# Two attention layers with MLPs on one core: the division by the softmax totals is moved from VectorE to ScalarE and GpSimd

## The chip, the cores and the metric

The kernel runs on one core of a Trainium2 chip. The time is the device time in microseconds (us) of one execution; several executions are timed and the median is given. A profile is one execution recorded by the hardware profiler, whose span runs from its first to its last instruction. The engines are named as in the profile: PE is TensorE (matmuls; PEld is its weight loads), DVE is VectorE, ACT is ScalarE, POOL is GpSimd, SP is SyncE, which here only issues transfers. [...]

## The reference

The input x has 4 sequences of 1024 rows of 256 numbers, all float32. Four blocks follow each other, each added to x after a layernorm.

```
x = x + attn_a(layernorm(x))   # 16 heads of 64, scale 1/(64*64*16), output weights WO
x = x + ffn(layernorm(x))      # 256 -> 1024, gelu, 1024 -> 256, with biases
x = x + attn_b(layernorm(x))   # own layernorm, low-rank q and k/v, rotary q and k, residual inside
x = x + ffn(layernorm(x))

# in both attention layers, for each sequence and head
scores = q @ k.T * scale
attn   = softmax(scores, axis=-1)
out    = attn @ v
```

The softmax is computed as exp(score - row maximum), and the division by the row's total is put off until after the product with v: out = (exp @ v) / total.

## The kernel before, in words

Each attention layer is cut into 32 pairs of heads (4 sequences, 8 pairs each) and each pair into 8 steps of 128 query rows, so there are 256 steps in a layer. The order on every engine is written out by hand in `steps_with` (L324): the loop over steps calls the stages of different steps in a fixed order, and each engine runs its instructions in the order in which they were issued.

A step s has these stages. `scores` (L229) makes the two heads' 128x1024 scores on TensorE, into one of three double banks. `exponentials` (L244) takes the row maximum on VectorE (L249) and the exponential on ScalarE (L251), with the row total as a by-product. `invert` (L257) takes the reciprocal of the totals on VectorE (L259), and ScalarE spreads it into a seventeenth column block of the probabilities (L260). `turn` (L265) transposes the probabilities in squares of 32x32 on VectorE (L271), the inverse totals along with them, into a buffer T.

Two steps make a half-pair h, called a round here (HB = 2). `send` (L282) moves T to a buffer pT in sixteen transfers that exchange the squares between partitions: eleven are issued by SyncE in the odd step, after the transpose, and five by GpSimd in the following even step. T and pT have two buffers each. Five steps after its first step (LAG = 5), `weigh` (L290) multiplies the exponentials in pT with v on TensorE (L297), into two banks of PSUM, one for each step of the round. Then `divide` (L303) multiplies each bank by the inverse totals, which are found in pT beside the exponentials (`pT[h][:, :, :, NK2, :]`), and writes oT (L307). When pT has been read there its buffer is free for the sends of the round two later. In the next, even step `project` (L312) multiplies oT with the output weights on TensorE (L167), ScalarE copies the result (`got`, L320), and GpSimd adds it to x (L322).

In an odd step TensorE runs the scores of the next step, then weigh; in the even step that follows it runs the scores of one more step and then project, with no other work between weigh and project than these scores. VectorE runs two maxima, the transpose, and in an odd step the division, before the next reciprocal.

Work for later pairs is spread as "pieces" over the steps: q, k and v of the next pair (copies of their banks on ScalarE, L535, L537, L548 in layer A, L640, L661 in B), and the layernorm and transposes of the next sequence (L147, L153, L156). In layer B the rotary embedding is such a piece: GpSimd issues two transfers that swap neighbouring rows of q or k (`change`, L645), in an odd step, and in the next even step it does three element-wise operations on 128x512 (`rotate`, L650 to L652). One such set falls into each round. GpSimd also adds the layernorm's result to x for the next sequence (L596), and b2 to x in the MLP (L388, 128x256).

In the names of the profile, `sc` is the scores, `p` the probabilities, `mm` a bank of PSUM for matmul results, and `nmax` the negated row maximum.

Of the kernel before, what the change touches and what calls it, by code (L numbers as in the profile page):

```python
# [11 lines left out]
ALU = mybir.AluOpType  # L12
# [13 lines left out]
SQ = 32  # L26
NG = P // SQ
HB = 2
# [5 lines left out]
NK2 = S // DH  # L34
# [5 lines left out]
def hybrid_block_kernel(  # L40
# [5 lines left out]
    nc = tc.nc  # L46
# [134 lines left out]
    def attention(prep_batch, prep_pair, wo, loader, lead):  # L181
# [22 lines left out]
        n = len(steps)  # L204
# [22 lines left out]
        sc, probs, total, T, pT, av, oT = {}, {}, {}, {}, {}, {}, {}  # L227

        def scores(s):  # L229
            g, qs = steps[s]  # L230
            qT, kT = tiles[g]["qT"], tiles[g]["kT"]
            for j in range(2):
                sc[s, j] = ps_sc.tile([P, S], F32, tag="sc", name="sc")
            for m in range(S // 512):
                for half in range(2):
                    for j in range(2):
                        rows = slice(j * DH, (j + 1) * DH)
                        nc.tensor.matmul(  # L238
                            sc[s, j][ts(half, DH), ts(m, 512)],
                            qT()[rows, ts(2 * qs + half, DH)], kT()[rows, ts(m, 512)],  # L240
                            start=True, stop=True,
                        )

        def exponentials(s, j):  # L244
            if j == 0:
                probs[s] = pp.tile([P, NK, NG, SQ], F32, tag="p", name="p")
                total[s] = small.tile([P, 2], F32, tag="total", name="total")
            nmax = small.tile([P, 1], F32, tag="nmax", name="nmax")
            nc.vector.tensor_reduce(nmax, sc[s, j], AX.X, ALU.max, negate=True)  # L249
            place = j ^ (s % HB)  # L250
            nc.scalar.activation(  # L251
                probs[s][:, :NK2, ts(j, 2), :],
                sc.pop((s, j)).rearrange("p (k c i) -> p k c i", c=2, i=SQ), AF.Exp,
                bias=nmax, accum_out=total[s][:, place : place + 1],
            )

        def invert(s):  # L257
            t = total.pop(s)
            nc.vector.reciprocal(t, t)  # L259
            nc.scalar.copy(  # L260
                probs[s][:, NK2].rearrange("p (j c) i -> p j (c i)", j=2),
                t.unsqueeze(2).to_broadcast([P, 2, DH]),
            )

        def turn(s):  # L265
            h, q = divmod(s, HB)
            if q == 0:
                T[h] = tp.tile([P, SENT], F32, tag="T", name="T").rearrange(
                    "p (c q k i) -> p c q k i", c=NG, q=HB, k=NK
                )  # L270
            nc.vector.transpose(  # L271
                T[h][:, :, q, :, :].rearrange("p c k i -> p k c i"), probs.pop(s)
            )
# [8 lines left out]
        def send(h, engine, which):  # L282
            if h not in pT:
                pT[h] = ptp.tile([P, SENT], F32, tag="pT", name="pT").rearrange(
                    "p (a q k i) -> p a q k i", a=NG, q=HB, k=NK
                )
            for a, c in which:
                engine.dma_start(pT[h][ts(c, SQ), a], T[h][ts(a, SQ), c])  # L288

        def weigh(h):  # L290

            v = tiles[HB * h // NT]["v"]()
            av[h] = [group(P) for q in range(HB)]
            for k in range(NK2):
                for q in range(HB):
                    for j in range(2):
                        nc.tensor.matmul(  # L297
                            av[h][q][ts(j ^ q, DH)], v[ts(j, DH), k, :],
                            pT[h][ts(j, DH), :, q, k, :],
                            start=(k == 0), stop=(k == NK2 - 1),  # L300
                        )

        def divide(h):  # L303
            oT[h] = otp.tile([P, HB, P], F32, tag="oT", name="oT")
            R = pT.pop(h)[:, :, :, NK2, :]
            for q, sums in enumerate(av.pop(h)):
                nc.vector.tensor_tensor(  # L307
                    oT[h][:, q].rearrange("p (a i) -> p a i", i=SQ),
                    sums.rearrange("p (a i) -> p a i", i=SQ), R[:, :, q], op=ALU.mult,
                )  # L310

        def project(h):  # L312
            g, t0 = divmod(HB * h, NT)
            b, pr = pairs[g]
            po = group(HB, D)
            for t in range(HB):
                paired(po[:, t, :], [(oT[h][:, t], [wos[g][:, t]] * 2)])
            oT.pop(h)
            got = tmp.tile([P, HB, D], F32, tag="tmp", name="got")
            nc.scalar.copy(got, po)  # L320
            xd = xs[b][:, t0 : t0 + HB, :]
            nc.gpsimd.tensor_add(xd, xd, got)  # L322

        def steps_with(others):  # L324
            for k, f in others:
                pieces.setdefault(k, []).append(f)
            for s in range(-1, n + LAG + 1):
                h, part = divmod(s - LAG, HB)
                ahead = 0 <= s + 1 < n
                if 0 <= s < n:  # L330
                    invert(s)
                if ahead:
                    scores(s + 1)
                if part == 1 and 0 <= s // HB - 1 < n // HB:
                    send(s // HB - 1, nc.gpsimd, squares[len(squares) - POOL_DMA :])
                    T.pop(s // HB - 1)
                if part == 1 and 0 <= h < n // HB:
                    project(h)
                if ahead:
                    exponentials(s + 1, 0)  # L340
                for f in pieces.get(s - EARLY, ()):
                    f()
                if part == 0 and 0 <= h < n // HB:
                    weigh(h)
                if ahead:
                    exponentials(s + 1, 1)
                if 0 <= s < n:
                    turn(s)
                if part == 0 and 0 <= h < n // HB:
                    divide(h)  # L350
                if part == 0 and 0 <= s < n:
                    send(s // HB, nc.sync, squares[: len(squares) - POOL_DMA])
                for f in pieces.get(s, ()):
                    f()
# [394 lines left out]
```

## Time and profile before

| | us |
|---|---|
| median of three runs | 3321.29 (3320.86 to 3324.8) |
| the profiled execution's own time | 3321.26 |
| its span | 3319.5 |
| VectorE busy | 2626.0 (79%) |
| ScalarE busy | 1892.7 (57%) |
| GpSimd busy | 1774.2 (53%) |
| the division, L307, 512 instructions | median 0.270 each |

The span has four parts: attention A up to about 1420 us, an MLP, attention B from about 1650 to 3090 us, and the last MLP. Busy shares are means over all four, so a stage is read from its own stretch. An instruction's row in a group gives its line, engine, operation, operands, shape and count, then busy time and mean duration, then the idle time of its engine ahead of it and what ended most of that idle time. A row of the timeline gives the start, the duration, the engine, the line and the operands, and in brackets how long the engine had been idle and what released it. The ends of matmuls are modelled by the profiler. TensorE can have matmuls in the records whose intervals overlap.

### The profile page before, as it was taken

Reading aid. Unit: us, or ns where it says so; the run is one execution under the profiler, and the core shown is the slowest. Engines: PE = TensorE matmul, PEld = TensorE weight load, DVE = VectorE, ACT = ScalarE, POOL = GpSimd, SP = SyncE. Lnnn points to the kernel's source line nnn. Section 1 sums busy time; section 2 is a strip of 40 time slices with the busy share of each in tenths; the row PEclk is TensorE's granted clock in tenths of the full one; section 3 lists DMA queues with packets and bytes.
Section 4 is the critical chain, followed back from the end, with each engine's and each line's share of the span. In section 5 each row is a group of like instructions: output and inputs, shape, how many; then the busy total and the mean of one; then the engine's idle time right before and its main releaser. Section 6 shows DMA issues by size and latency. Waiting matters only on the chain.

```text
span 3319.5 us, 124467 instructions
## 1 busy us (share of the span) xinstructions
PE 3241.7 (98%) x52608; PEld 2028.1 (61%) x52608; DVE 2626.0 (79%) x2898; ACT 1892.7 (57%) x3664; POOL 1774.2 (53%) x2482
## 2 busy tenths in 40 slices
PE   8999999999999999999999999999999999998999
PEld 4666666666666666666655655656556656665666
DVE  7998998899988999931069988999899989999100
ACT  5666666665666666643356665666566666665332
POOL 3444444344444444321257887888778878886100
PEclk9999999999999999999999999999999999999999
DMA  8888888888888888830049888998899889998100
GB/s 225 224 218 218 223 224 219 219 220 222 228 212 221 220 225 222 221 82 0 7 126 243 240 241 242 250 248 242 232 247 251 241 235 251 251 254 228 41 20 19
DMA packets 250825, 659.82 MB, mean 199 GB/s; under 512 B 76352, under 2 KB 105024, under 8 KB 250272
## 3 DMA queue, kind: packets, MB, share of 16 engines
q1 hardware_dynamic: 167248, 415.43, 48.0%
q0 software_dynamic: 83024, 236.44, 25.2%
q8 instruction: 418, 6.85, 0.9%
q14 instruction: 135, 1.11, 0.1%
HBM read 43.39 MB, written 4.19 MB: 14 GB/s over the span
## 4 chain that ended last, share of the span: by engine, by line
PE 70%; DVE 9%; SPq 7%; DMA 6%; issue 3%; ACT 3%; POOL 1%; DVEq 0%; ACTq 0%; POOLq 0%
PE sc L238 20%; PE mm L297 18%; PE mm L167 14%; PE mm L413 7%; SPq L288 7%; PE ph L402 6%; DVE T L271 5%; DMA pT<-T 5%; PE mm L176 4%; DVE nmax L249 3%; ACT p L251 1%; PE mm L153 1%; POOL pT L288 1%; DVE oT L307 0%; ACT gT L406 0%
## 5 line engine op out<-in xcount | busy, mean ns | idle before, releaser
L249 DVE TENSOR_REDUCE nmax<-sc 128x1 f32<-128x1024 f32 x1024 | 1202.8, 1216 | 171.1 <-PE sc L238 161.1
L251 ACT ACTIVATE p<-sc,nmax 128x1024 f32<-128x1024 f32 x1024 | 1144.0, 1117 | 329.1 <-DVE nmax L249 328.2
L271 DVE STREAM_TRANSPOSE T<-p 128x2176 f32<-128x2176 f32 x512 | 1246.7, 2435 | 62.2 <-DMA pT<-T 46.8
L288 POOL DMA_DIRECT2D pT<-T x1280 | 625.3, 496 | 1016.8 <-DVE total L259 775.9
L238 PE MATMUL sc<-kT,qT 64*64 64x512 f32 x8192 | 1109.9, 599 | 18.1 <-ACT p L251 15.3
L297 PEld LDWEIGHTS mm<-pT,v 64*64 64x64 f32 x32768 | 960.1, 133 | 159.2 <-issue 105.1
L297 PE MATMUL mm<-pT,v 64*64 64x128 f32 x32768 | 1009.4, 270 | 12.8 <-issue 11.2
L238 PEld LDWEIGHTS sc<-kT,qT 64*64 64x64 f32 x8192 | 347.4, 133 | 408.6 <-issue 276.5
L260 ACT COPY p<-total 128x128 f32<-128x128 f32 x512 | 152.8, 298 | 509.5 <-DVE total L259 503.1
L322 POOL TENSOR_TENSOR x<-x,got 128x512 f32<-128x512 f32 x256 | 330.5, 1291 | 49.4 <-ACT got L320 45.4
L420 DVE TENSOR_TENSOR x<-x,mm 128x512 f32<-128x512 f32 x32 | 21.9, 686 | 364.7 <-PE mm L413 364.7
L167 PE MATMUL mm<-wo,oT 128*64 128x256 f32 x2048 | 277.8, 392 | 13.4 <-DVE oT L307 12.3
L167 PEld LDWEIGHTS mm<-wo,oT 128*64 128x64 f32 x2048 | 124.3, 136 | 260.4 <-DVE oT L307 151.1
L320 ACT COPY got<-mm 128x512 f32<-128x512 f32 x256 | 150.0, 586 | 226.4 <-PE mm L167 225.5
L406 ACT ACTIVATE gT<-ph,b_sb 128x512 f32<-128x512 f32 x128 | 87.5, 686 | 304.3 <-PE ph L402 304.3
L167 PE MATMUL mm<-hT,w 128*64 128x512 f32 x1024 | 243.7, 597 | 1.0 <-ACT hT L156 1.0
L413 PE MATMUL mm<-w_sb,gT 128*128 128x256 f32 x1024 | 226.0, 381 | 6.6 <-ACT hT L156 6.6
L402 PE MATMUL ph<-hT,w_sb 128*128 128x512 f32 x512 | 229.2, 600 | 0.0
L413 PEld LDWEIGHTS mm<-w_sb,gT 128*128 128x128 f32 x1024 | 193.1, 190 | 39.4 <-ACT hT L156 9.4
L251 ACT ACTIVATION_READ_ACCUMULATOR p<-sc,nmax 128x1 f32 x1024 | 204.4, 200 | 0.0
L388 POOL TENSOR_TENSOR x<-x,b_sb 128x256 f32<-128x256 f32 x64 | 44.5, 726 | 275.2 <-ACT xn L147 275.2
L176 PEld LDWEIGHTS mm<-w,hT 128*64 128x64 f32 x4096 | 140.9, 138 | 71.3 <-issue 69.7
(88 smaller groups left out, 2187.5 us busy)
## 6 DMA issues: line engine op xcount, KB each, us to landing
pT<-T SPq DMA_DIRECT2D x2816, 136.0 KB, 4.7
pT<-T POOLq DMA_DIRECT2D x1280, 136.0 KB, 4.6
turned<-kT POOLq DMA_DIRECT2D x128, 128.0 KB, 3.8
turned<-qT POOLq DMA_DIRECT2D x128, 128.0 KB, 3.9
w<-in_wqkv_a POOLq DMA_DIRECT2D x96, 128.0 KB, 6.1
wo<-in_wo_a POOLq DMA_DIRECT2D x32, 128.0 KB, 5.2
wo<-in_wo_a POOLq DMA_DIRECT2D x64, 64.0 KB, 5.6
wo<-in_wo_b SPq DMA_DIRECT2D x32, 128.0 KB, 4.5
```

What stands on the lines that cost most here:

```text
L167: nc.tensor.matmul(out[ts(j, DH)], lhsT[:, ts(j, DH)], rhs[j], start=(first and i == 0), stop=(last and i == len(parts) - 1),)
L176: nc.tensor.matmul(out[ts(j, DH)], lhsT, rhs[:, ts(j, DH)], start=(i == 0), stop=(i == len(parts) - 1),)
L238: nc.tensor.matmul(sc[s, j][ts(half, DH), ts(m, 512)], qT()[rows, ts(2 * qs + half, DH)], kT()[rows, ts(m, 512)], start=True, stop=True,)
L249: nc.vector.tensor_reduce(nmax, sc[s, j], AX.X, ALU.max, negate=True)
L251: nc.scalar.activation(probs[s][:, :NK2, ts(j, 2), :], sc.pop((s, j)).rearrange("p (k c i) -> p k c i", c=2, i=SQ), AF.Exp, bias=nmax, acc ...
L260: nc.scalar.copy(probs[s][:, NK2].rearrange("p (j c) i -> p j (c i)", j=2), t.unsqueeze(2).to_broadcast([P, 2, DH]),)
L271: nc.vector.transpose(T[h][:, :, q, :, :].rearrange("p c k i -> p k c i"), probs.pop(s))
L288: engine.dma_start(pT[h][ts(c, SQ), a], T[h][ts(a, SQ), c])
L297: nc.tensor.matmul(av[h][q][ts(j ^ q, DH)], v[ts(j, DH), k, :], pT[h][ts(j, DH), :, q, k, :], start=(k == 0), stop=(k == NK2 - 1),)
L322: nc.gpsimd.tensor_add(xd, xd, got)
L402: nc.tensor.matmul(ph, w1_sb[:, c, ts(f, P)], hT[n][:, c, :], start=(c == 0), stop=(c == NC - 1),)
L413: nc.tensor.matmul(po[n][:, t % 2, :], gT[n][:, f, ts(t, P)], w2_sb[:, f, :], start=(f == 0), stop=(f == NF - 1),)
```

## The change

`divide` becomes `take`. ScalarE copies the two banks to oT as they are, and one multiply on GpSimd, over both halves and in place, brings in the inverse totals. The buffer pT is then freed by GpSimd. In the order of the step, `take` is called ahead of `turn` instead of behind it; since `turn` issues on VectorE only, this decides nothing between the two. On ScalarE the two copies stand behind the step's second exponential and ahead of the integer-numbered pieces of the step; on GpSimd the multiply stands ahead of those pieces, the swap transfers L645 among them. Below line 310 the line numbers of the kernel after are lower by one.

```diff
-        def divide(h):
+        def take(h):
+
             oT[h] = otp.tile([P, HB, P], F32, tag="oT", name="oT")
-            R = pT.pop(h)[:, :, :, NK2, :]
             for q, sums in enumerate(av.pop(h)):
-                nc.vector.tensor_tensor(
-                    oT[h][:, q].rearrange("p (a i) -> p a i", i=SQ),
-                    sums.rearrange("p (a i) -> p a i", i=SQ), R[:, :, q], op=ALU.mult,
-                )
+                nc.scalar.copy(oT[h][:, q], sums)
+            parts = oT[h].rearrange("p q (a i) -> p a q i", i=SQ)
+            nc.gpsimd.tensor_mul(parts, parts, pT.pop(h)[:, :, :, NK2, :])
...
                 if ahead:
                     exponentials(s + 1, 1)
+                if part == 0 and 0 <= h < n // HB:
+                    take(h)
                 if 0 <= s < n:
                     turn(s)
-                if part == 0 and 0 <= h < n // HB:
-                    divide(h)
                 if part == 0 and 0 <= s < n:
                     send(s // HB, nc.sync, squares[: len(squares) - POOL_DMA])
```

## The prediction

> **What bounds the kernel now.** I read the page's first part, the windows by stage, the waits of TensorE in each attention layer, the timeline of single rounds, and the groups. A round is two steps: two transposes (L271), one weigh (L297), one division (L307), one projection (L167 from oT). Layer A runs from 60 to 1420 us, layer B from 1690 to 3060 us.
>
> The page, then two stretches of the windows, one in each layer (columns: PE, PEld, DVE, ACT, POOL busy us with instruction counts, clock, DMA share, GB/s):
>
> ```profile
> PE 3241.7 (98%) x52608; PEld 2028.1 (61%) x52608; DVE 2626.0 (79%) x2898; ACT 1892.7 (57%) x3664; POOL 1774.2 (53%) x2482
> ...
> 460.00:860.00 400.00, 399.12 (x7648) 252.83 (x7644) 362.24 (x365) 243.45 (x485) 168.96 (x271) 1.00 0.84 221
> 2080.00:2480.00 400.00, 390.83 (x7007) 240.97 (x7003) 364.84 (x370) 248.74 (x485) 325.75 (x418) 1.00 0.90 243
> ```
>
> In layer A TensorE leaves 0.9 us of 400 idle: VectorE, at 91%, is not what ends a round. In layer B TensorE leaves 9.2 us, VectorE is as full, DMA is at 0.90 and GpSimd at 81%, DMA issues included. The waits of TensorE, layer A first, then B (us, times, longest):
>
> ```profile
> PE mm L297 <- issue: 5.5, 10, 1.2
> PE sc L238 <- ACT p L251: 0.3, 1, 0.3
> PE mm L167 <- DVE oT L307: 0.2, 1, 0.2
> ...
> PE sc L238 <- ACT p L251: 13.0, 13, 2.9
> PE mm L167 <- DVE oT L307: 11.6, 27, 0.5
> ```
>
> The wait that the change bears on, a projection for oT, costs 0.2 us in layer A and 11.6 us in B. So a gain is small; the question is whether the new chain makes this wait large. One round of layer A, from the timeline:
>
> ```profile
> 801.01 3.67 PE L297 MATMUL mm<-pT,v 64*64 64x128 f32 x128
> 803.63 1.12 ACT L251 ACTIVATE p<-sc,nmax 128x1024 f32<-128x1024 f32 x1
> 804.50 1.90 PE L238 MATMUL sc<-kT,qT 64*64 64x512 f32 x16
> 804.64 0.19 ACT L251 ACTIVATION_READ_ACCUMULATOR p<-sc,nmax 128x1 f32 x1
> 805.87 0.45 DVE L307 TENSOR_TENSOR oT<-mm,pT 128x128 f32<-128x128 f32 x2
> 806.33 1.08 PE L167 MATMUL mm<-wo,oT 128*64 128x256 f32 x8
> 806.61 2.46 POOL L288 DMA_DIRECT2D pT<-T  x5 [4.79 <-DVE total L259]
> ```
>
> Let W be the end of a weigh (804.68). TensorE then has only sixteen score matmuls before the projection, which starts at W+1.65. Division starts at W+1.19, after the transpose, and ends at W+1.64. Over the 123 rounds of layer A the medians are the same: first projection load W+1.64, division end W+1.64. The first projection needs only the first half, done 0.18 us earlier. So oT may come 0.2 us later than now before TensorE stalls, and not more. ScalarE is free at W+0.15, GpSimd long before W (median W-4.4).
>
> **The change part by part.** *Removed from VectorE:* 512 multiplies, 0.45 us a pair, 256 pairs: 115 us of its 2626. In A TensorE covers it, worth nothing. The reciprocal (L259) moves up 0.45 us, but the next maximum (L249) waits for scores that end at W+1.72.
>
> *Added to ScalarE:* two 128x128 copies out of PSUM per round. Rows, none with 128 columns from PSUM:
>
> ```profile
> L320 ACT COPY got<-mm 128x512 f32<-128x512 f32 x256 | 150.0, 586 | 226.4 <-PE mm L167 225.5
> L548 ACT COPY v<-mm 128x256 f32<-128x256 f32 x128 | 47.5, 373 | 0.0
> L260 ACT COPY p<-total 128x128 f32<-128x128 f32 x512 | 152.8, 298 | 509.5 <-DVE total L259 503.1
> L388 POOL TENSOR_TENSOR x<-x,b_sb 128x256 f32<-128x256 f32 x64 | 44.5, 726 | 275.2 <-ACT xn L147 275.2
> ```
>
> The first two fall by 213 ns per 256 columns, so 128 columns come to 0.27 us (L260: 0.30). ScalarE's neighbours overlap by 0.10 us, so the pair takes 0.44. Got (L320) starts 0.10 us after its matmul; the exponentials free ScalarE at W+0.15. Copies: W+0.13 to W+0.57. Behind them in ScalarE's queue stand the copy of the inverse (L260), which waits for VectorE until W+1.35 anyway, and, in a few odd steps, a standardisation (L147, 0.6 us) that used to run first. The banks come free earlier than under the division.
>
> *Added to GpSimd:* one 128x256 multiply, in place. The nearest row is L388, 726 ns; 128x512 adds (L322) and multiplies (L650) are within 20 ns of each other, so the operation does not matter. The pattern in runs of 32 elements is not in the trace: I bound it by 0.69 us (L388's start-to-start spacing) and the 128x512 row, 1.29, and take 0.73. Start 0.08 us after ScalarE (the shortest gap from L320 to L322).
>
> *The signal from GpSimd to TensorE* is in no row. Bounds: 0.03 us (VectorE's division to the load) and 0.29 us (from L652 to the transfer L645 that waits for it); from L651 to L652, which also waits, it is 0.08 us. I take 0.1. The Trainium skill, Perfetto Trace Analysis, section GPSIMD Engine Instruction, has GpSimd's reported end at the acknowledged write, with the semaphore visible only after that, and calls such a span unreliable. By the rows oT comes at W+0.57+0.08+0.73+0.10 = W+1.48, in time; with the page's caution read as the 0.29 us row, at W+1.67, which costs 0.02 us a round.
>
> *Shared port.* The same skill, SBUF — State Buffer, section Who interferes with whom, says that GpSimd blocks fully against a VectorE instruction in a two-port mode. VectorE's transpose runs until W+1.2 here. If it held the port, oT would come near W+2.1, at +0.4 us a round, some 100 us in all. The rows speak against it: L650 to L652 take 1.255 to 1.295 us each with transposes beside them. I count nothing.
>
> *Moved on GpSimd's queue.* The multiply waits for W, and everything behind waits with it. Layer A has room (idle 4.8 us before the sends). Layer B, one round with W = 2008.42:
>
> ```profile
> 2005.85 1.27 POOL L652 TENSOR_TENSOR kT<-kT,turned 128x512 f32<-128x512 f32 x1
> 2007.41 1.13 POOL L645 DMA_DIRECT2D turned<-kT  x2 [0.29 <-POOL kT L652]
> 2010.35 2.43 POOL L288 DMA_DIRECT2D pT<-T  x5 [1.81 <-DVE total L259]
> 2012.80 1.29 POOL L322 TENSOR_TENSOR x<-x,got 128x512 f32<-128x512 f32 x1
> 2014.05 1.27 POOL L650 TENSOR_TENSOR kT<-kT,cos_sb 128x512 f32<-128x512 f32 x1
> ```
>
> The swap transfers (L645) go from W-1.0 to W+1.4, the five sends from W+1.9 to about W+2.6, the add to W+5.0, the rotation to W+6.4 and its end to W+10.2. The next multiply can run at W+10.65 at the earliest, in a light round of 10.0 us (projection to projection, 1953.10 to 1963.12). So it fits, with 0.4 us to spare. The swap lands 3.8 us (median; 5.9 at most) after issue, the rotation needs it 4 us after: just covered. SyncE's eleven sends per round wait for the slot of pT and start where they do now, or 0.2 us earlier.
>
> *Layer B.* Gain: the 11.6 us of waits for oT, where VectorE was late, go; of the 13.0 us for exponentials I give 5, since VectorE catches up sooner. Loss: in ten rounds L652 ends later than W+0.5 already, at W+0.5 to W+2.1; adding the multiply and signal to each end and taking what exceeds W+1.65 gives 11 us.
>
> **Sum**: A 0, B -12 -5 +11 = -6 us on the profiled execution's 3321.26 us (span 3319.5 and 1.8 around it), the same as the median of 3321.29: 3315 us.
>
> **The rivals.** *In time, little moves* (0.45): as summed, 3305 to 3322; half of it beyond 0.2% (6.6 us, about what a measurement can tell from no change).
>
> *VectorE relieved in layer B* (0.12): in 37 of 125 rounds VectorE waits under 0.15 us for anything. Shedding 0.45 us there is 17 us, with the 25 us of both waits 40: 3282 to 3305. Against it: 48 us of VectorE's idle time in B lies before the transpose, most of it for transfers of pT (38.7 us), at a DMA share of 0.90, and a light round has a loop without VectorE (scores, projection, got, exponential, scores, weigh) that already takes 10.0.
>
> *oT late in every round* (0.31), the case on the other side: the multiply in pieces, or GpSimd's signal, takes more than assumed. It decides at W+1.65. At W+1.84 (multiply 1.1 us) the excess over all rounds is 26 us in A and 28 more than now in B: 3370 or so with B's relief; at W+1.67 it is about 10 us, 3330. The upper bounds together (1.29 and 0.29, W+2.22) give 141 us; I weigh the lower part most.
>
> *GpSimd's queue binds in B* (0.12): twelve rounds carry two adds L596 (0.73 us each), 10.9 us of work against 10.0 to 10.4; or the rotation waits for its swap. With 0.1 to 0.3 us in each of 125 rounds, 12 to 38 us: 3327 to 3353.
>
> **How the numbers follow.** Faster: 0.12 + half of 0.45 = 0.35. Same: 0.22. Slower: the last two, 0.43. The range cuts the far ends of the second and third case: 3294 to 3358. The likeliest case alone: 3305 to 3322.
>
> **What would show it.** Right: the multiply near 0.73 us, ending near W+1.4; the wait of L167 for GpSimd under 5 us in A; A's rounds still 10.75 us. Wrong: a multiply above 0.9 us, or projections starting after W+1.7 in every round of A; L645 or L650 idle for long in B. VectorE falls by 115 us in any case.

## The result and the profile after

The kernel after takes 3333.6 us (median of 19 runs, 3327.99 to 3341.47), the one before 3324.8 on the same chip (19 runs, 3318.61 to 3329.5). The ratio is 1.0028, 95% interval 1.002 to 1.0035: 9 us slower, where 3315 and a gain were forecast. The time lies inside the range that was given, 3294 to 3358, but on the other side of the kernel before. The profiled executions have spans of 3327.1 and 3319.5 us, so the profiles show 7.6 us of it.

The page of after, in its parts for busy time, for the chain that ended last, and for the group of the new multiply:

```profile
PE 3242.7 (97%) x52608; PEld 2020.4 (61%) x52608; DVE 2529.1 (76%) x2386; ACT 1988.0 (60%) x4176; POOL 1958.6 (59%) x2738
...
PE 69%; SPq 15%; DMA 6%; ACT 4%; issue 3%; DVE 2%; POOL 1%; DVEq 0%; ACTq 0%; POOLq 0%
PE sc L238 19%; PE mm L297 18%; SPq L288 14%; PE mm L167 14%; PE mm L412 7%; PE ph L401 6%; DMA pT<-T 5%; PE mm L176 4%; ACT p L251 2%; DVE nmax L249 1%; DVE T L271 1%; POOL oT L309 1%; SPq L628 0%; PE mm L153 0%; ACT gT L405 0%
...
L309 POOL TENSOR_TENSOR oT<-oT,pT 128x256 f32<-128x256 f32 x256 | 186.1, 727 | 762.5 <-ACT oT L307 656.3
```

The same part for the chain in the page of before:

```profile
PE 70%; DVE 9%; SPq 7%; DMA 6%; issue 3%; ACT 3%; POOL 1%; DVEq 0%; ACTq 0%; POOLq 0%
PE sc L238 20%; PE mm L297 18%; PE mm L167 14%; PE mm L413 7%; SPq L288 7%; PE ph L402 6%; DVE T L271 5%; DMA pT<-T 5%; PE mm L176 4%; DVE nmax L249 3%; ACT p L251 1%; PE mm L153 1%; POOL pT L288 1%; DVE oT L307 0%; ACT gT L406 0%
```

VectorE is relieved as meant, and its share of the chain falls from 9% to 2%. But SyncE's issuing of the sends (SPq L288) rises from 7% to 14%, although the change does not touch a send. The chain of e2 below, with the change in layer B alone, shows 15%, that of e1, with the change in layer A alone, 7%. The multiply takes the 727 ns that were assumed, and GpSimd's oT is 1% of the chain.

The two stretches of the windows, one in each layer, in the columns of before:

```profile
460.00:860.00 400.00, 398.72 (x7602) 252.09 (x7596) 348.10 (x293) 257.77 (x561) 198.34 (x311) 1.00 0.86 221
2080.00:2480.00 400.00, 392.23 (x6989) 239.93 (x6985) 351.07 (x297) 262.56 (x560) 349.46 (x454) 1.00 0.88 244
```

TensorE is about as full in both stretches; the loss is not even over layer B. From the first projection of a layer to its last, layer A went from 1397.5 to 1390.7 us (-6.8) and layer B from 1372.6 to 1387.0 (+14.4). Together that is the 7.6 us of the profiles. A gained, where nothing was counted, and B lost, where a gain was.

The waits of TensorE in after, layer A first (us, times, longest):

```profile
PE mm L167 <- POOL oT L309: 0.3, 1, 0.3
PE sc L238 <- ACT p L251: 0.3, 1, 0.3
```

and in layer B the waits of VectorE, TensorE and GpSimd:

```profile
DVE nmax L249 <- PE sc L238: 94.1, 126, 3.2
DVE T L271 <- DMA pT<-T: 45.7, 25, 4.7
...
PE mm L167 <- POOL oT L309: 16.5, 34, 2.2
PE sc L238 <- ACT p L251: 14.3, 12, 2.9
...
POOL kT L649 <- DMA turned<-kT: 10.9, 13, 1.6
POOL qT L649 <- DMA turned<-qT: 10.4, 12, 1.7
```

VectorE's waits in layer B of before:

```profile
DVE nmax L249 <- PE sc L238: 51.3, 71, 3.0
DVE T L271 <- DMA pT<-T: 38.7, 29, 3.2
```

The new chain is in time in A: one late projection in the whole layer. In B the wait for oT grows from 11.6 to 16.5 us. All of VectorE's idle time ahead of a transpose grows more, from 48 to 69 us in B, most of it for transfers out of T. Of the 20 us some is scatter: e1, e12 and e16 below, whose layer B is that of before, have 50 to 62 us; after, e2 and e4 have 67 to 70. Its longer wait for scores is the room that the division left, and is harmless by itself.

One round of layer B in after shows how the delays follow each other (W, the end of the weigh, is 2501.23):

```profile
2501.61 0.42 ACT L307 COPY oT<-mm 128x128 f32<-128x128 f32 x2
2502.11 0.72 POOL L309 TENSOR_TENSOR oT<-oT,pT 128x256 f32<-128x256 f32 x1 [1.01 <-DMA pT<-T]
2502.77 1.13 POOL L644 DMA_DIRECT2D turned<-qT  x2
...
2503.90 2.43 POOL L288 DMA_DIRECT2D pT<-T  x5
...
2506.35 1.29 POOL L321 TENSOR_TENSOR x<-x,got 128x512 f32<-128x512 f32 x1
...
2508.56 0.40 PE L297 MATMUL mm<-pT,v 64*64 64x128 f32 x2 [0.80 <-DMA pT<-T]
2509.30 1.27 POOL L649 TENSOR_TENSOR qT<-qT,cos_sb 128x512 f32<-128x512 f32 x1 [1.66 <-DMA turned<-qT]
...
2510.02 2.44 DVE L271 STREAM_TRANSPOSE T<-p 128x2176 f32<-128x2176 f32 x1 [4.67 <-DMA pT<-T]
```

Here the second exponential lasts to W+0.4, so the copies and the multiply come late by that, and the swap (L644 now) can only be issued at W+1.54. The multiply's bracket names a DMA, but what it waits for last are the copies, which end at 2502.03, 0.08 us ahead of it. GpSimd's five sends follow at W+2.67 and the rotation (L649) stands 1.66 us for the swap to land. The transpose waits 4.67 us for sends of earlier rounds to leave T.

What happens to the transfers in B shows best against the end of a round's second transpose, which is at W+1.25 in the median of both kernels. The table is worked out from the traces: medians over 116 rounds of layer B, in us, but for the swaps over all 128, and for the last two rows a mean and a count; the three columns on the right are experiments told below.

| | before | after | e3, swap first | e6, tiny wait | e9, tiny wait, swap first |
|---|---|---|---|---|---|
| swap issued | -1.97 | 0.02 | -1.97 | 0.99 | -1.61 |
| swap landed | 2.56 | 4.39 | 2.58 | 5.73 | 3.10 |
| GpSimd's first send issued | 0.67 | 1.15 | 0.61 | 2.27 | 1.25 |
| SyncE's first send issued | 0.40 | 1.04 | 0.66 | 1.40 | 0.56 |
| SyncE's last send landed | 12.87 | 13.24 | 13.48 | 14.10 | 13.79 |
| sum of SyncE's 11 issue times, mean | 8.36 | 8.86 | 8.42 | 9.12 | 8.88 |
| pauses of SyncE between rounds under 0.35 us, of 115 | 15 | 38 | 9 | 36 | 26 |

Before, the swaps were issued in the last 2 us ahead of the sends, in SyncE's median pause of 2 us between two rounds. Now their 2 x 128 KB start with the sends. SyncE takes 0.5 us longer to issue the same eleven sends and in 38 rounds instead of 15 goes from one round's sends straight into the next. Both go with the change in B from profile to profile: e1, e12 and e16 have 8.43 to 8.48 us and 14 to 19 such rounds, e2, e4 and e11 8.84 to 8.94 us and 36 to 39. But a longer issue is not a loss by itself: in layer A the sum rises as well with the change, from 8.31 to 8.60 us, and A gets shorter.

### The profile page after: what moved, and what is told of

Its sections match the earlier page's. It is cut to its first block, busy times and chain, and to the rows that moved or that the text cites. A ratio compares the mean times of both kernels' runs of the same rounds, so it can differ in the third digit from the quotient of the medians.

```text
span 3327.1 us, 125678 instructions
## 1 busy us (share of the span) xinstructions
PE 3242.7 (97%) x52608; PEld 2020.4 (61%) x52608; DVE 2529.1 (76%) x2386; ACT 1988.0 (60%) x4176; POOL 1958.6 (59%) x2738
## 4 chain that ended last, share of the span: by engine, by line
PE 69%; SPq 15%; DMA 6%; ACT 4%; issue 3%; DVE 2%; POOL 1%; DVEq 0%; ACTq 0%; POOLq 0%
PE sc L238 19%; PE mm L297 18%; SPq L288 14%; PE mm L167 14%; PE mm L412 7%; PE ph L401 6%; DMA pT<-T 5%; PE mm L176 4%; ACT p L251 2%; DVE nmax L249 1%; DVE T L271 1%; POOL oT L309 1%; SPq L628 0%; PE mm L153 0%; ACT gT L405 0%
## 5 line engine op out<-in xcount | busy, mean ns | idle before, releaser
L288 POOL DMA_DIRECT2D pT<-T x1280 | 629.5, 499 | 118.0 <-PE sc L238 55.9
L309 POOL TENSOR_TENSOR oT<-oT,pT 128x256 f32<-128x256 f32 x256 | 186.1, 727 | 762.5 <-ACT oT L307 656.3
```

Source lines behind the costliest of these rows:

```text
L309: nc.gpsimd.tensor_mul(parts, parts, pT.pop(h)[:, :, :, NK2, :])
```

## The experiments

All were timed in sets beside the kernel before, whose median in these sets was 3322.82 to 3325.18 us. "A" and "B" are the lengths of the layers in the profiled execution, from the first projection to the last. One profile's A scatters between 1396.8 and 1406.1 over seven kernels that have the division of before there and no tiny wait (before, e2, e4, e5, e7, e10, e13), and B between 1372.6 and 1379.4 over the four whose layer B is that of before with nothing added or left out (before, e1, e12, e16), so small differences are read from the medians. In the code below, `lead` is 3 in layer A and 5 in layer B, and what stands behind a # was added for this text.

| run | median us | ratio (95% interval) | A | B |
|---|---|---|---|---|
| e1_a_only | 3318.38 | 0.9986 (0.9979 to 0.9992) | 1391.5 | 1379.4 |
| e2_b_only | 3337.46 | 1.0045 (1.0032 to 1.0058) | 1400.3 | 1396.0 |
| e3_swap_first | 3332.22 | 1.0032 (1.002 to 1.0044) | 1390.8 | 1390.6 |
| e4_both_beside | 3341.14 | 1.0057 (1.0045 to 1.0068) | 1401.6 | 1389.0 |
| e5_mult_beside | 3329.27 | 1.0015 (1.0008 to 1.0023) | 1406.1 | 1370.0 |
| e6_tiny_wait | 3366.87 | 1.014 (1.0122 to 1.0159) | 1406.5 | 1409.6 |
| e7_copies_beside | 3325.78 | 1.001 (1.0002 to 1.0018) | 1401.1 | 1380.4 |
| e8_four_sends | 3356.24 | 1.01 (1.0084 to 1.0116) | 1388.0 | 1421.1 |
| e9_tiny_wait_swap_first | 3366.09 | 1.0114 (1.0098 to 1.013) | 1403.0 | 1401.8 |
| e10_before_no_add | 3314.42 | 0.9969 (0.9958 to 0.998) | 1400.7 | 1367.9 |
| e11_after_no_add | 3326.43 | 1.0003 (0.9993 to 1.0012) | 1392.5 | 1385.3 |
| e12_a_only_filled | 3319.59 | 0.9985 (0.9976 to 0.9994) | 1394.0 | 1374.1 |
| e13_before_no_swap | 3303.24 | 0.9942 (0.9929 to 0.9956) | 1396.8 | 1355.7 |
| e14_after_no_swap | 3292.66 | 0.9911 (0.9899 to 0.9924) | 1394.1 | 1351.9 |
| e15_tiny_wait_no_swap | 3323.76 | 0.9999 (0.999 to 1.0007) | 1406.2 | 1368.4 |
| e16_a_only_six | 3328.93 | 1.0014 (1.0007 to 1.0022) | 1402.6 | 1373.9 |
| e17_swap_on_sync | 3391.31 | 1.0195 (1.0176 to 1.0213) | 1393.3 | 1450.9 |
| e18_swap_on_sync_seven | 3345.18 | 1.0061 (1.0046 to 1.0076) | 1390.8 | 1399.3 |

**Each layer alone.** e1 has the change in layer A and the division of before in B; e2 the other way round (`lead == 5`). Both keep `divide` and add `take`.

```diff
...
+                if part == 0 and 0 <= h < n // HB and (lead == 3):
+                    take(h)
                 if 0 <= s < n:
                     turn(s)
-                if part == 0 and 0 <= h < n // HB:
+                if part == 0 and 0 <= h < n // HB and not (lead == 3):
                     divide(h)
```

> The division is moved to ScalarE and GpSimd in attention layer A only; layer B keeps the division on VectorE. In the profile of the changed kernel the last projection of layer A comes 6.9 us sooner than before and layer B takes 14.5 us longer. If the two layers act apart: 0.998 of before, some 7 us faster, with layer B's 1372 us unchanged within its scatter of 5 us. If the gain of layer A was one execution's scatter: 1.000.

> The move in layer B only. If the two layers act apart: 12 to 16 us slower than before, ratio 1.004 to 1.005. If layer B's loss comes from a state that layer A hands on: near 1.000.

The layers act apart: -0.14% and +0.45% add to +0.31%, beside +0.28% for both. The change in A alone, e1, beats both kernels: 3318.38 us, about 5 us under before, interval clear of 1. By the medians, too, the change costs layer B about 14 us (e2 14.2 us over before).

**The swap put ahead of the multiply** (e3, from after):

```diff
-                    work += [(k + 1, lambda i=i, qb=qb: change(i, qb))]
+                    work += [(k + 1 - EARLY, lambda i=i, qb=qb: change(i, qb))]
```

> The changed kernel, but on GpSimd's queue the two swap transfers of layer B stand ahead of the multiply instead of behind it, so that they are issued about 2.4 us earlier, and the five sends 1.1 us earlier. Theory of late transfers (the multiply waits for the weigh and holds back GpSimd's transfers, which then collide with SyncE's sends): layer B's loss goes, total near 3318, 7 us or more below before. Theory of the late multiply (the rotation keeps GpSimd busy past the weigh): layer B keeps its loss, as the rotation stands ahead of the multiply in both, 3328 or more. Theory that ScalarE's copies come late behind the exponentials: loss kept too.

The waits in layer B of e3:

```profile
DVE T L271 <- DMA pT<-T: 45.0, 33, 3.0
...
PE mm L167 <- POOL oT L309: 26.4, 41, 3.2
```

The swap is back at its old time, and SyncE's issue time and pauses are too (the table above). But the multiply now stands behind the end of the rotation and the swap, at W+0.90 in the median instead of W+0.60, the wait for oT rises from 16.5 to 26.4 us, and pT comes free later as well: SyncE waits 22.1 us in 30 rounds of B for the multiply to free it, against 7.9 us in 8 rounds of after, and its first send is still at 0.66. The time is the same as that of after, and so is VectorE's idle time ahead of the transposes, 69 us. The forecast of the theory of late transfers, near 3318, failed in this run, and that of the late multiply held. On GpSimd's queue either the swap or the multiply is late, and this run can't tell what a late swap costs alone.

**The load without the wait, the wait without the load.** e4 keeps VectorE's division, adds the two copies to a spare tile on ScalarE and multiplies that on GpSimd; the projection waits for none of it. e5 adds a GpSimd multiply of constants of the same size, which takes 0.62 us instead of the 0.73 that its expectation counts, and e7 the two copies alone.

```diff
...
+            for q, sums in enumerate(av[h]):          # e4 and e7
+                nc.scalar.copy(spare[:, q], sums)
+            flat = spare.rearrange("p q i -> p (q i)")  # e4
+            nc.gpsimd.tensor_mul(flat, flat, b2_sb)
...
+                    nc.gpsimd.tensor_mul(spare.rearrange("p q i -> p (q i)"), b2_sb, b2_sb)  # e5, behind divide(h)
```

> The kernel before with its division on VectorE, and beside it two copies of the same banks on ScalarE to a tile that nobody reads, and a multiply of that tile on GpSimd at the place where the changed kernel has its own. The projection does not wait for these. Theory of late transfers: layer B loses at least its 14 us, since the multiply waits for the weigh and holds back GpSimd's transfers as in the change. Theory of the late multiply: the projection is not held, so layer B loses under 5 us. Layer A unchanged in both, within 3 us.

> The kernel before with its division on VectorE, and a 128x256 multiply of constants on GpSimd, which waits for nothing, at the place of the changed kernel's multiply. It adds 0.73 us to GpSimd's queue per round and moves no wait: the swap transfers go out at about W-0.3 instead of W-1.0, the sends where they did. Theory of late transfers: within 4 us of before. Theory that GpSimd's queue is full in layer B and any further work shows: 8 us or more slower.

> The kernel before with its division on VectorE, and beside it the two copies of the banks on ScalarE to a tile that nobody reads; GpSimd as before. Theory of late transfers and of a full GpSimd queue: within 3 us of before. Theory that ScalarE's two copies (0.43 us a round) delay the exponentials of layer B, and with them the scores: 8 us or more slower.

With oT made by VectorE as before, e4 loses 0.57%, and its swaps and sends are as late as those of after (swap at 0.02, SyncE's first send at 1.04). So the loss does not need the new way of oT to the projection. The multiply alone, which waits for nothing, and the copies alone, which keep GpSimd free, cost 0.15% and 0.10%: the load has a price, but the smaller one. e5's 6 us lie between its two forecasts (within 4, 8 or more), and in its profile layer B is not longer than before, 1370.0 us.

e6 adds the wait with next to no load, a 128x1 multiply at the place of the multiply. It waits for VectorE's division, so longer than after's multiply waits.

```diff
...
                     divide(h)
+                    nc.gpsimd.tensor_mul(spare, oT[h][:, 1, :1], eps)
```

> The kernel before, and on GpSimd at the same place a multiply of one column (128x1) that reads oT and so waits for the division, W+1.65. It adds about 0.2 us of work, but holds the swap transfers back to about W+1.8 and the sends to W+3.0, later than the change does. Theory of late transfers: 10 us or more slower, all of it in layer B. Theory of a full queue: under 4 us.

The waits of VectorE and GpSimd in layer B of e6 (its lines are shifted: L273 is the transpose, L353 the new operation, L648 the swap; for the division that L353 waits for, the row names the reciprocal L261, which VectorE runs right behind it):

```profile
DVE T L273 <- DMA pT<-T: 43.7, 33, 2.9
DVE T L273 <- DMA wo<-in_wo_b: 16.7, 12, 2.5
...
POOL spare L353 <- DVE total L261: 149.3, 94, 6.0
POOL turned L648 <- POOL spare L353: 36.4, 109, 0.3
```

An operation of 0.19 us costs 1.4%. In 109 rounds the swap waits right behind it. Layer B is 37 us longer than in before. Not all of the loss may lie there, as was expected: layer A is 9 us longer too, at the upper end of its scatter. This is the clearest sign of where to look: not what GpSimd does, but what stands behind its wait.

e9 puts the swap ahead of that tiny operation, with the edit of e3.

> The kernel before with the same 128x1 GpSimd multiply that waits for the division, but the swap transfers L645 now stand ahead of it in GpSimd's queue. The add L322, the rotation and the five sends still stand behind it; nothing on the path waits for its result. Theory 1, the held-back swap is what costs: its transfers go back to about W-1.0, and the time falls from 3367 to about 3322 to 3330 (ratio 1.000 to 1.002). Theory 2, the held-back sends and adds cost by themselves: still 3345 to 3367 (ratio over 1.006).

The first theory fell in that form: 1.0114. The second held. The swap is nearly back (-1.61), but the wait still holds GpSimd's sends from 0.67 to 1.25, with the add and the rotation behind them. A late swap is thus not the only thing that a wait on this queue can cost.

**SyncE with one send more** (e8, from after, POOL_DMA = 4, so twelve sends on SyncE):

> The changed kernel with four instead of five of the sixteen sends of a round on GpSimd and twelve on SyncE. GpSimd is relieved of 0.5 us a round, SyncE gets one send more (about 0.8 us of some 9.5 us). If GpSimd's queue is the cause of layer B's loss: 3 to 8 us faster than the change, 3325 to 3330. If SyncE's stream of sends is the tighter one: slower than the change, 3340 or more, and layer A slower too.

It is 1.0% slower than before and layer B 34 us longer than in after; layer A is not longer, against what was expected (1388.0 beside 1390.7 us). VectorE's and TensorE's waits for the sends in its layer B:

```profile
DVE T L271 <- DMA pT<-T: 71.3, 27, 5.6
...
PE mm L297 <- DMA pT<-T: 16.5, 10, 3.0
```

SyncE has no room in B: with one send more on it the layer gets 34 us longer.

**Room on GpSimd.** e10 is before and e11 after, both without the add L322 in layer B.

```diff
-            nc.gpsimd.tensor_add(xd, xd, got)
+            if lead == 3:
+                nc.gpsimd.tensor_add(xd, xd, got)
```

> The kernel before without GpSimd's add L322 in layer B: x does not take up the second attention's output, and each round of B has 1.29 us less on GpSimd. It is the base for the next run. If GpSimd's load already cost something in the kernel before, layer B gets shorter by 5 to 20 us; if it has room there, within 3 us of 3323.

> The kernel after without the same add in layer B, so that GpSimd has about 9.5 us of work in a round of 10.0 to 10.4 us. Theory 1, a full GpSimd queue is what makes the change lose in B: the multiply and the swap find it free, and this kernel is at most 2 us over the one before without the add, or below it by A's 5 to 7 us. Theory 2, the swap's place behind the wait for the weigh costs with room on GpSimd too: layer B stays 10 to 14 us longer than that of the kernel before without the add.

e10 is itself 11 us faster than before, so GpSimd's add has a price in B already without the change. With 1.29 us per round of room the change still loses 12 us (3326.43 - 3314.42), layer B 17 us. In e11 GpSimd waits much for the swap:

```profile
DVE T L271 <- DMA pT<-T: 49.6, 31, 5.8
...
POOL kT L650 <- DMA turned<-kT: 59.9, 51, 2.7
POOL qT L650 <- DMA turned<-qT: 45.7, 44, 2.4
```

It stands 106 us at the rotation, five times as long as in after, and the loss is no larger. So neither a full queue nor the rotation's wait for its swap is what loses; theory 2 held.

**Without the swap transfers.** e13 is before, e14 after and e15 the tiny wait of e6, all without the transfers L645.

```diff
-                for r in range(2):
-                    nc.gpsimd.dma_start(turned[i, qb][r::2], made[i, qb][1 - r :: 2])
...
-                nc.gpsimd.tensor_mul(other, other, sin_sb[:, ts(qb, QB)])
+                nc.gpsimd.tensor_mul(other, straight, sin_sb[:, ts(qb, QB)])
```

> The kernel before without the swap transfers L645 in layer B: the rotation multiplies the unswapped rows by the sines, with the same three GpSimd operations. The base for the next two. It takes 1.1 us of issue from GpSimd and about 256 KB of transfers from each round, so layer B gets shorter by 5 to 25 us if transfers bound it.

> The kernel after, also without the swap transfers. Nothing that moves data stands right behind the multiply; GpSimd's sends wait for the transpose in both kernels. Theory 1, the swap held back behind the wait for the weigh is what costs in B: layer B is at most 3 us longer than that of the kernel before without swaps, and the whole is 3 to 10 us shorter for A's gain. Theory 2, the loss comes from elsewhere (late copies, the later add and rotation): layer B stays 10 us or more longer.

> The kernel before with the 128x1 GpSimd multiply that waits for the division, and without the swap transfers. What the wait holds back now is the five sends (by 0.6 to 0.8 us) and the adds and rotation behind them. If held-back sends cost by themselves: layer B 15 us or more longer than without the wait, and A 4 us longer as in the two runs with this wait. If the swap was what counted: B within 5 us.

The waits of layer B in e13:

```profile
DVE T L271 <- DMA pT<-T: 8.4, 6, 2.9
...
PE mm L167 <- DVE oT L307: 4.5, 10, 0.5
```

and in e14:

```profile
DVE T L271 <- DMA pT<-T: 13.2, 7, 3.2
...
PE mm L167 <- POOL oT L309: 6.3, 14, 1.0
```

This is the pair that decides. Without swaps the change gains: 3292.66 against 3303.24, 10.6 us, and the runs of the two do not overlap (3292.19 to 3296.43, and 3300.21 to 3308.49). Layer B is 3.8 us shorter with the change, less than the scatter of single profiles, where it is 14.4 longer with swaps. The wait for oT rises by under 2 us. So the change's loss in B hangs on the swaps, which in after stand behind the multiply. That they lose by running into the sends is the reading of the traces in the table above, in which late swaps and a slower SyncE go together; only their part in the loss is shown by the run itself. The pair also takes the swaps' traffic (the DMA share between 2080 and 2480 us falls from 0.90 in before to 0.85 in both) and 1.13 us of issue from GpSimd; e11 shows that room on GpSimd alone does not do it. Nor does the room without swaps hide every delay, as e15 shows.

The tiny wait still costs 20.5 us without swaps (3323.76 - 3303.24), 43.6 with them (3366.87 - 3323.25, the median of before in that set). So the wait costs with no swap behind it: GpSimd's first send is at 1.38 in B instead of 0.67, B is 12.7 us longer than in e13, a little under the 15 that were expected, and A, which never had swaps, 9.4. The add and the rotation, which also stand behind the wait, are moved with the sends and not told apart from them. After's multiply by itself does not hold back the sends: in e14, without swaps, GpSimd's first send is at 0.59 in B.

**The swap taken off GpSimd, its traffic kept.** e17 is after with the swaps issued by SyncE ahead of its sends; e18 also gives GpSimd seven sends of the sixteen in B, so that SyncE has eleven transfers a round again.

```diff
-                    nc.gpsimd.dma_start(turned[i, qb][r::2], made[i, qb][1 - r :: 2])
+                    nc.sync.dma_start(turned[i, qb][r::2], made[i, qb][1 - r :: 2])
...
-                    work += [(k + 1, lambda i=i, qb=qb: change(i, qb))]
+                    work += [(k + 1 - EARLY, lambda i=i, qb=qb: change(i, qb))]
```

> The kernel after with the two swap transfers issued by SyncE ahead of its sends of the round, in place of GpSimd. The wait for the weigh no longer stands in front of them and GpSimd has 1.13 us less to issue, but SyncE issues 13 transfers in a round of B. If the swap's place behind the wait is all that loses in B and SyncE's 2 us between rounds take the swap: at or under the change in layer A alone, 3310 to 3319. If SyncE's stream has no room for 1.2 us more: sends start late, VectorE waits longer for T, 3330 to 3350.

> The same with seven of the sixteen sends on GpSimd in layer B, so that SyncE issues eleven transfers in a round, as before, and GpSimd one transfer's issue less than the change needed before. If SyncE's count of issues was what cost in the run beside it: 3308 to 3320. If sends on GpSimd cost by themselves, as the sixth one in layer A did: no better than the run beside it.

Neither wins, and both are outside what was expected: e17 is slower than its slower forecast, and e18 lies between its two. With thirteen issues on SyncE layer B is 64 us longer than in after. The waits in layer B of e18:

```profile
DVE T L271 <- DMA pT<-T: 14.8, 19, 1.8
...
PE mm L167 <- POOL oT L309: 45.4, 37, 3.4
```

In e18 the transfers are better than in the kernel before: VectorE's wait for pT<-T falls to 14.8 us, and all its idle time ahead of a transpose from 48 to 37 us. The loss has gone over to oT, 45.4 us in 37 projections, as GpSimd has seven sends ahead of the add and the rotation, and comes late to the multiply: in 41 rounds of B it starts over 0.15 us after the copies, in after in 18. The swap's lateness can be cured; room for the multiply at the right moment of GpSimd's round was not found with the swaps there.

**A's gain.** e12 is e1 with two 128x128 multiplies of constants on VectorE at the division's old place in layer A. e16 is e1 with six sends on GpSimd in layer A.

```diff
...
+                if part == 0 and 0 <= h < n // HB and lead == 3:   # e12
+                    for q in range(HB):
+                        nc.vector.tensor_tensor(spare[:, q], ident, ident, op=ALU.mult)
...
-                    send(s // HB, nc.sync, squares[: len(squares) - POOL_DMA])
+                    send(s // HB, nc.sync, squares[: len(squares) - POOL_DMA - (lead == 3)])   # e16, and the rest on GpSimd
```

> The change in layer A alone, with two 128x128 multiplies of constants on VectorE at the place where the division stood in layer A, so that VectorE has the same load as before there while SyncE's sends still wait for the transpose alone. Theory 1, A gains because VectorE is relieved of 0.45 us a round: the gain goes, 3323 (ratio 1.000). Theory 2, A gains because SyncE's sends start 0.27 us earlier: the gain stays, 3317 to 3319 (ratio 0.9985).

> The change in layer A alone, and there six of the sixteen sends on GpSimd, so that SyncE issues ten; layer B as before. Theory 1, A's gain came from SyncE's sends starting 0.27 us earlier, so SyncE's stream matters in A: another 2 to 8 us shorter than with the change in A alone, 3310 to 3317. Theory 2, SyncE has room in A: within 2 us of 3318.5, or longer if GpSimd's sixth send lands late.

The stretch of layer A in the windows of e12, columns as before:

```profile
460.00:860.00 400.00, 398.67 (x7630) 252.42 (x7624) 364.47 (x367) 257.41 (x558) 197.22 (x307) 1.00 0.86 221
```

VectorE is as busy as before (364 of 400 us; 348 in after), and the gain stays: 0.9985 beside 0.9986. A's gain is not VectorE's relief. SyncE's first send does start 0.27 us earlier in A (0.13 after the transpose instead of 0.40), because pT is free by then, but the last one does not land earlier (12.62 instead of 12.42), and e16, which shortens SyncE's share, lost 10 us against e1, while e8, which lengthens it, has no longer layer A. The theory of earlier sends is what was left over, and no run supports it. Some 2 to 3 us of A's gain lie in its last rounds: the round that begins at 1417 us in before takes 19.4 to 20.2 us in before, e2, e7, e10 and e13, and 16.4 to 18.1 in after, e1, e3, e11, e12 and e14. The rest is spread thin. Its cause stays open.

## Why the prediction was wrong, point by point

**The sizes of the new operations held.** Copies of 0.27 us, from W+0.09 to W+0.53 (forecast W+0.13 to W+0.57), multiply 727 ns, oT at W+1.38 (forecast W+1.48). The signal from GpSimd to TensorE takes 0.05 us in the rounds in which TensorE waits for it, under the 0.1 taken, and the caution of the Trainium skill (Perfetto Trace Analysis, GPSIMD Engine Instruction) cost nothing here: GpSimd's reported end could be used as it stands. Nor did the rule on the shared port (SBUF — State Buffer, Who interferes with whom) show: the multiply takes 712 to 740 ns beside transposes. The rival that held 0.31, oT late in every round, did not occur.

**VectorE's relief** is 115.3 us of rows, as said; the engine's busy time falls by 97, since neighbours overlapped. It is worth nothing in A, as forecast: e12 shows that.

**Layer A at 0** was -7 in the profile, and -5 by the median of e1. The step called TensorE full and looked no further; where the gain comes from stays open.

**Layer B's three terms**, -12 -5 +11, were about waits for oT and exponentials. These went from 11.6 to 16.5 and from 13.0 to 14.3 us, so +6 in place of -6. The +11 held: read round by round, projections start late by 9.7 us in ten rounds in which GpSimd is still busy. The -12 did not: in 28 other rounds they are late by another 9.7 us with the copies, which stand behind a late exponential on ScalarE. The -5 came out as +1.3.

**The step that failed is the one costed at nothing**: "The swap lands 3.8 us (median; 5.9 at most) after issue, the rotation needs it 4 us after: just covered", and SyncE's sends "start where they do now, or 0.2 us earlier". The move itself was seen, W-1.0 to W+1.4 (-0.6 to +1.3 in the medians). It was then judged by the one reader of the swap, the rotation. The traffic that the swap moved into was not asked about: sends at a DMA share of 0.90, which the profile showed, and a SyncE stream with a pause of 2 us per round, which it held and the prediction did not read. SyncE's sends in B start 0.64 us later, not earlier. With swaps B is 14.4 us longer with the change, without them 3.8 shorter; the difference, 18 us of single profiles, measures the missing term as well as these runs can. By medians it is 8.8 + 10.6 = 19 us. Shown is that the change's loss in B depends on the swaps; that they lose by way of SyncE's stream is read from the traces and not tried apart, and with the swaps in time and the multiply late (e3) the loss is as large.

**The rival that GpSimd's queue binds** gave the right time (3327 to 3353), but not the way; that the time fits is luck. It named GpSimd's total load, or the rotation's wait for its swap. e11 has room for the first and five times more of the second, and loses as much.

## What to carry to other kernels

When an in-order queue gets an operation that waits, list every transfer issue behind it and ask where each one lands in the stream of the other transfers, not only whether its reader still gets it in time. A 0.19 us operation with a wait cost 1.4% here, a 0.62 us one without a wait 0.15%. Where two layers share code, try the change in each alone: here the half that gains (0.9986) was hidden by the half that loses.

## What the runs showed of the hardware

In no row of before or after does GpSimd read a bank of PSUM; in after ScalarE's copies bring it the results of weigh. A GpSimd multiply of 128x256 that goes through its operands in runs of 32 elements takes 727 ns, the same as a contiguous one (e4), and TensorE starts 0.05 us after its reported end where it waits for it. With one tile as both inputs the contiguous multiply took 616 ns (e5). SyncE's time to issue the same eleven sends is not fixed: 8.36 us a round of B before, 8.86 in after and 9.12 in e6. In layer B it is longer in the kernels whose swaps or GpSimd sends start later, near SyncE's own; in layer A, without swaps, it rises with the change from 8.31 to 8.60 us. What in the transfers' path stretches an issue was not tried. The two 128 KB swaps of a round, with their issue on GpSimd, cost 20 us over layer B even at the place that they have in before (e13 against before).
